# PSUM banks for the experts of a two-layer kernel: gates, ups, logits and transposes apart, projections in two banks, six row buffers, later output stores

## The chip, the cores and the metric

The kernel runs on one core of one Trainium2 chip, as one program that computes two layers. The metric is the device time of one execution in microseconds (us); the median of three runs is compared.

## The reference, cut to what matters

The program has many stages. The change touches the last one, which takes `x` of shape (8, 512, 256), runs a tanh recurrence over its 512 time steps, and feeds the states to a mixture of 16 experts, of which each token uses two:

```python
xW = jnp.einsum('ntd,dh->nth', x, Wx) + b
def step(h_prev, xw_t):
    h_next = jnp.tanh(xw_t + h_prev @ Wh)
    return (h_next, h_next)
_, hs = jax.lax.scan(step, h0, jnp.swapaxes(xW, 0, 1))
...
def _mlp(x, wg, wu, wd):
    return jnp.einsum('bsi,id->bsd', jax.nn.silu(x @ wg) * (x @ wu), wd)
router_logits = jax.nn.sigmoid(x @ gate_w + gate_b)
expert_values, expert_indices = jax.lax.top_k(router_logits, k=TOP_K)
expert_values = expert_values / jnp.sum(expert_values, axis=-1, keepdims=True)
...
return x + _mlp(x, shared_wg, shared_wu, shared_wd) + expert_weighted
```

The second `x` is the recurrence's output, and `expert_weighted` is the sum of the two chosen experts' `_mlp`, each times its value. The layer's input is added once more. All of it is in 32-bit floats.

## The kernel before, in words

The last stage is `rnn_moe` (L1565). Its loop over the 512 steps issues a step of the recurrence (`rnn_step`, L1262) and then at most one piece of other work on TensorE. In a step, TensorE (PE) multiplies the state with `wh` (L1273) into one of two small tiles `pg` and seeds the next step's tile with the projected input (L1257); ScalarE (ACT) takes the tanh (L1277); VectorE (DVE) transposes the result into `ring` (L1278), from which the next step's matmuls read. So a step is a loop PE, ACT, DVE, PE.

The order is written out by hand for PE, ACT and DVE (`manual_schedule`, L1664). Generators yield 1 when they have put a piece on PE and 0 when not. What a piece leaves for ACT and DVE goes into `later`, and `consume()` (L1630) issues it in the next step, behind that step's tanh and transpose. The kinds of pieces are:

- `rnn_project` (L1238): the input's projection for 16 time steps, 31 times, two pieces each. Both matmuls (L1247) accumulate into `px`; DVE adds the bias into `xw` (L1249).
- `chunk` (L1312): for 16 finished time steps (128 tokens), 32 times. The logits' matmul (L1327) and two transposes (L1337) write one tile `po`, the logits in columns 256 to 271, the transposes in columns 0 to 255; DVE and ACT turn the logits into `rl` (L1331, L1332), ACT copies the transposed rows to `hr` (L1342). Then come the shared expert's gate (L1348, L1350) and up (L1352), both into halves of one tile `pw`, ACT's sigmoid and DVE's two multiplies (L1356, L1357, L1361), and the down projection with the residual (L1365, L1369).
- `rank` (L1382): after a block of chunks (blocks of 6, 8, 11 and 7), DVE ranks the tokens by expert, and GpSimd (POOL) scatters the rows to a buffer `xs` in device memory, grouped by expert in tiles of 128 rows (L1455).
- `tiles` (L1467): 27, 31, 37 and 29 tiles for the four blocks, 124 in all, three pieces each: gate, up, down. `fetch` (L1473) loads a tile's expert weights `w` (384 KB) and rows `x` (128 KB) on SP's queue. `turn` (L1480) transposes half of the next tile's rows in the same piece as a gate or an up; `gate(m, 0)` and `gate(m, 1)` (L1490) write the gate and the up of tile m into the two halves of one tile `pg` of tag `gu` (L1493, L1496). ACT's sigmoid (L1501) and DVE's multiply (L1502) read the gate, DVE's second multiply reads the up (L1509). `down` (L1511) multiplies with the third weight; ACT copies the result to `y` (L1517), and SP stores it to `ys` (L1518).
- `collect` (L1541): POOL gathers each token's two rows from `ys` (L1550), DVE adds them to `acc` with their values (L1558), and SP stores `acc` to the output (L1562), 32 stores in all.

A chunk's piece goes first, otherwise a tile's (L1674). Gathers and scatters advance beside it. When the steps are over, the rest runs without them (L1678); this is called the tail here. Of the 124 tiles, 65 have had their store issued when the recurrence ends.

PSUM pools, each tile a whole bank: `psx` one (L1611), the recurrence two (L1612), `pxt` one for the row transposes (L1616), `pgu` two for gates and ups (L1617), `pd` two for `po`, `pd` and `py` (L1618). That is all eight. Dependencies are kept by bank: an instruction that writes a bank waits for all that read it before, whatever the columns.

SP and POOL are not in the hand-written order: a scheduler places their instructions by when buffers come free. Weights have seven buffers (`M.wp`, L1607), rows four (`M.sp`, L1606), the gathered rows six. Each DMA of SP's also waits for the eighth DMA before it.

Of the kernel before, what the change touches and what calls it, by code (L numbers as in the profile page):

```python
# [9 lines left out]
F32 = mybir.dt.float32  # L10
I32 = mybir.dt.int32
U32 = mybir.dt.uint32
AF = mybir.ActivationFunctionType
# [5 lines left out]
P = 128  # L19
B = 8  # L20
S = 512
D = 256
# [1215 lines left out]
def rnn_project(K, M):  # L1238

    ahead = chunk_x(K, M, 1, "xp")  # L1240
    for n in range(1, S // XB):
        xc = ahead
        if n + 1 < S // XB:
            ahead = chunk_x(K, M, n + 1, "xp")
        px = M.psx.tile([P, D], F32, name="px", tag="px")
        for k in range(2):
            K.nc.tensor.matmul(px, xc[:, k], M.wx[:, k, :], start=(k == 0), stop=(k == 1))  # L1247
            if k == 1:
                M.later(lambda n=n, px=px: K.nc.vector.tensor_tensor(M.xw[:, n, :], px, M.rbias, ALU.add))  # L1249
            yield 1  # L1250
# [30 lines left out]
class Experts:  # L1281
# [30 lines left out]
    def chunk(self, c, ring):  # L1312

        K, M, NE = self.K, self.M, self.NE
        nc, mm, later = K.nc, K.nc.tensor.matmul, M.later
        t0 = (self.first + c) * XB
        hT = M.hp.tile([P, 2, B, XB], F32, name="hT", tag="hT")
        for k in range(2):
            nc.gpsimd.tensor_copy(hT[:, k], ring[:, :, k, 0:B].rearrange("p t b -> p b t"))
        xc = chunk_x(K, M, t0 // XB, "xc")  # L1320
        hk = [hT[:, k].rearrange("p b t -> p (b t)") for k in range(2)]
        yield 0
        yield 0
        po = M.pd.tile([P, D + NE], F32, name="po", tag="pd")
        pr, pt = po[:, D:], po[:, 0:D].rearrange("p (k t) -> p k t", k=2)
        for k in range(2):
            mm(pr, hk[k], M.wr[:, k, :], start=(k == 0), stop=(k == 1))  # L1327
        rl = M.sp.tile([P, NE], F32, name="rl", tag="rl")

        def logits():  # L1330
            nc.vector.tensor_tensor(rl, pr, M.rb, ALU.add)  # L1331
            nc.scalar.activation(rl, rl, AF.Sigmoid)  # L1332

        later(logits)
        yield 1
        for k in range(2):
            nc.tensor.transpose(pt[:, k, :], hk[k], K.ident)  # L1337
        hr = M.ap.tile([P, D], F32, name="hr", tag="hr", bufs=16)
        self.hr.append(hr)

        def turned():
            nc.scalar.copy(hr, po[:, 0:D])  # L1342
            nc.vector.max(out=self.top[:, c, :], in_=rl)
            nc.vector.max_index(out=self.topi[:, c, :], in_max=self.top[:, c, :], in_values=rl)

        later(turned)
        pw = M.pgu.tile([P, 2, P], F32, name="pw", tag="gu")
        mm(pw[:, 0], M.wg[:, 0, :], hk[0], start=True, stop=False)  # L1348
        yield 1
        mm(pw[:, 0], M.wg[:, 1, :], hk[1], start=False, stop=True)  # L1350
        for k in range(2):
            mm(pw[:, 1], M.wu[:, k, :], hk[k], start=(k == 0), stop=(k == 1))  # L1352
        a = M.sp.tile([P, P], F32, name="a", tag="a")

        def act():
            nc.scalar.activation(a, pw[:, 0], AF.Sigmoid)  # L1356
            nc.vector.tensor_tensor(a, pw[:, 0], a, ALU.mult)  # L1357

        later(act)
        yield 1  # L1360
        later(lambda: nc.vector.tensor_tensor(a, pw[:, 1], a, ALU.mult))  # L1361
        yield 0
        yield 0
        pd = M.pd.tile([P, D], F32, name="pd", tag="pd")
        mm(pd, a, M.wd, start=True, stop=False)  # L1365
        yield 1
        pj = pd.rearrange("p (j k r) -> p k j r", j=4, k=2)
        for k in range(2):
            mm(pj[:, k], xc[:, k], K.ident, start=False, stop=(k == 1))  # L1369
        acc = M.ap.tile([P, D], F32, name="acc", tag="acc", bufs=27)  # L1370
        self.acc.append(acc)
        later(
            lambda: nc.vector.tensor_tensor(
                acc.rearrange("p (j k r) -> p j k r", j=4, k=2),
                pd.rearrange("p (j k r) -> p j k r", j=4, k=2),
                hr.rearrange("p (k j r) -> p j k r", j=4, k=2),
                ALU.add,
            )
        )
        yield 1  # L1380
# [86 lines left out]
    def tiles(self):  # L1467

        K, M, NT = self.K, self.M, self.NT
        nc, mm, later = K.nc, K.nc.tensor.matmul, M.later  # L1470
        W, X, G, A, T = {}, {}, {}, {}, {}

        def fetch(m):  # L1473
            W[m] = M.wp.tile([P, 768], F32, name="w", tag="w")
            row = nc.sync.value_load(self.wrow[0:1, m : m + 1], min_val=0, max_val=(self.NE - 1) * P)
            nc.sync.dma_start(out=W[m], in_=M.experts[bass.ds(row, P), :])
            X[m] = M.sp.tile([P, D], F32, name="x", tag="x")
            nc.sync.dma_start(out=X[m], in_=self.xs[m * P : (m + 1) * P, :])

        def turn(m, k):  # L1480
            if k == 0:
                T[m] = M.pxt.tile([P, 2, P], F32, name="pt", tag="xt"), M.sp.tile([P, 2, P], F32, name="xT", tag="xT")
            pt, xT = T[m]
            nc.tensor.transpose(pt[:, k, :], X[m][:, k * P : (k + 1) * P], K.ident)
            later(lambda: nc.scalar.copy(xT[:, k, :], pt[:, k, :]))
            if k == 1:
                T.pop(m)
                X[m] = xT

        def gate(m, g):  # L1490

            if g == 0:
                G[m] = M.pgu.tile([P, 2, P], F32, name="pg", tag="gu")  # L1493
            pg = G[m]
            for k in range(2):
                mm(pg[:, g], W[m][:, k * D + g * P : k * D + (g + 1) * P], X[m][:, k, :], start=(k == 0), stop=(k == 1))  # L1496
            if g == 0:
                a = A[m] = M.sp.tile([P, P], F32, name="ea", tag="ea")

                def silu():  # L1500
                    nc.scalar.activation(a, pg[:, 0], AF.Sigmoid)  # L1501
                    nc.vector.tensor_tensor(a, pg[:, 0], a, ALU.mult)  # L1502

                later(silu)
            else:
                X.pop(m)
                G.pop(m)
                a = A[m]
                later(lambda: nc.vector.tensor_tensor(a, pg[:, 1], a, ALU.mult))  # L1509

        def down(m):  # L1511
            py = M.pd.tile([P, D], F32, name="py", tag="pd")
            M.last = mm(py, A.pop(m), W.pop(m)[:, 2 * D : 3 * D], start=True, stop=True)

            def keep():
                y = M.sp.tile([P, D], F32, name="y", tag="y")
                nc.scalar.copy(y, py)  # L1517
                nc.sync.dma_start(out=self.ys[m * P : (m + 1) * P, :], in_=y)  # L1518

            later(keep)  # L1520

        for m in range(3):
            fetch(m)
        for k in range(2):
            turn(0, k)
        yield 1
        for m in range(NT + 1):
            for n in range(3):
                if n < 2 and m < NT:
                    gate(m, n)  # L1530
                    if m + 1 < NT:
                        turn(m + 1, n)
                    yield 1
                if n == 2:
                    if m:
                        down(m - 1)
                    if m + 3 < NT:
                        fetch(m + 3)
                    yield 1

    def collect(self):  # L1541

        K, M, nc = self.K, self.M, self.K.nc
        C, Y = self.C, {}
        for c in range(C + 2):
            for i in range(2):
                if c < C:
                    y = Y[c, i] = M.sp.tile([P, D], F32, name="yg", tag="yg", bufs=6)
                    self.paced(
                        nc.gpsimd.indirect_dma_start(  # L1550
                            out=y, out_offset=None, in_=self.ys[:, :], in_offset=bass.IndirectOffsetOnAxis(ap=self.row[:, c, i : i + 1], axis=0)
                        )
                    )
                    for _ in range(2 if M.left else 0):
                        yield 0
                if c > 1:
                    acc = self.acc[c - 2]
                    nc.vector.scalar_tensor_tensor(acc, Y.pop((c - 2, i)), self.tw[:, c - 2, i : i + 1], acc, ALU.mult, ALU.add)  # L1558
                yield 0
            if c > 1:  # L1560
                t0 = (self.first + c - 2) * XB
                nc.sync.dma_start(out=M.out[:, t0 : t0 + XB, :], in_=acc)  # L1562
# [293 lines left out]
```

## Time and profile before

| | us |
|---|---|
| median of 3 runs | 4574.04 (4570.07 to 4579.55) |
| the profiled execution | 4707.05 |
| its span, first to last instruction | 4705.1 |
| recurrence in it, first to last tanh | 3774.3 to 4515.8 |
| tail in it | 4516 to 4705 |
| busy in the span: PE | 3502.3 (74%) |
| busy in the span: DVE | 2148.3 (46%) |
| busy in the span: ACT | 1313.6 (28%) |
| busy in the span: POOL | 897.2 (19%) |

The profile is of one execution, longer than the timed ones, and covers all stages. For this change its totals say little; the stage has to be cut out by windows. A group is named by its line in the kernel, its engine, and output and inputs by tile. "PEld" is the weight load that precedes a matmul. A wait is written as the instruction that waited and the one that released it. A 32-bit matmul stands as two records, so "x4" is two matmuls.

### The profile page before, as it was taken

To read this page: it belongs to the slowest core of one execution; us is meant where nothing else is said; L and a number is where in the kernel's file an instruction comes from. 1 tells how busy PE (TensorE), PEld (TensorE's weight loads), DVE (VectorE), ACT (ScalarE), POOL (GpSimd) and SP (SyncE) were. 2 spreads that over 40 slices of the span, in tenths; PEclk is the share of its full clock that TensorE was granted. 3 is DMA by queue.
4 is the path that set the end of the run, shared out by engine and by line. 5 is a ranking of instruction groups with operands and counts; after the bars stand their busy time and mean duration, and the time that the engine had idled before them with its cause. 6 is when DMAs were issued, how large, how long until landed. Compare 5 with 4: busy or idle time off the path is not lost.

```text
span 4705.1 us, 122302 instructions
## 1 busy us (share of the span) xinstructions
PE 3502.3 (74%) x51550; PEld 2195.2 (47%) x51550; DVE 2148.3 (46%) x7641; ACT 1313.6 (28%) x4703; POOL 897.2 (19%) x1534
## 2 busy tenths in 40 slices
PE   8700067777766767578889999999999977888685
PEld 5500044444444444345545555555555545656464
DVE  3300045555554444434547666667666622332332
ACT  2100012222222222133434334433433311323132
POOL 0077500000000000042102222222222211020312
PEclk9855589999999999989999999999999987989698
DMA  2100000000000000100000000000000021333267
GB/s 77 37 1 1 0 16 17 17 17 12 12 3 3 3 3 3 54 26 19 9 2 1 1 1 1 1 1 1 1 1 1 7 88 45 115 113 107 88 202 216
DMA packets 103895, 155.55 MB, mean 33 GB/s; under 512 B 21264, under 2 KB 73776, under 8 KB 102960
## 3 DMA queue, kind: packets, MB, share of 16 engines
q1 hardware_dynamic: 72064, 108.46, 7.6%
q0 software_dynamic: 18432, 23.28, 1.7%
q10 hardware_dynamic: 12848, 15.99, 1.0%
q8 instruction: 404, 6.62, 0.6%
q14 instruction: 147, 1.20, 0.1%
HBM read 107.82 MB, written 41.02 MB: 32 GB/s over the span
## 4 chain that ended last, share of the span: by engine, by line
PE 53%; DVE 21%; ACT 9%; another core or an unknown queue 7%; issue 7%; DMA 1%; ACTq 1%; POOL 0%; SPq 0%; DVEq 0%; POOLq 0%
PE pga L629 9%; PE pg L1273 5%; DVE G L635 4%; PE pe L1107 4%; PE po L1161 3%; PE pg L1496 3%; PE pt L1146 3%; PE pp L1074 3%; ACT X L636 3%; PE pv L1092 3%; ACT th L645 2%; PE px L1177 2%; DVE pr L641 2%; DVE ring L646 2%
## 5 line engine op out<-in xcount | busy, mean ns | idle before, releaser
L629 PE MATMUL pga<-wh,ring 128*8 128x192 f32 x8176 | 427.8, 327 | 382.7 <-DVE ring L646 367.6
L629 PEld LDWEIGHTS pga<-wh,ring 128*8 128x8 f32 x8176 | 172.0, 88 | 633.1 <-DVE ring L646 579.1
L1278 DVE STREAM_TRANSPOSE ring<-h 128x64 f32<-128x64 f32 x512 | 125.6, 245 | 524.3 <-ACT h L1277 509.6
L635 DVE STREAM_TRANSPOSE G<-pga 128x192 f32<-128x192 f32 x512 | 196.5, 384 | 364.6 <-PE pga L629 364.6
L1127 ACT ACTIVATE sm<-sm,nm 128x388 f32<-128x388 f32 (+3 forms) x512 | 283.6, 555 | 252.4 <-DVE nm L1123 250.9
L636 ACT ACTIVATE X<-G 128x48 f32<-128x48 f32 x512 | 124.1, 242 | 813.5 <-DVE G L635 806.2
L441 PE MATMUL pA<-ohl,ohh 128*32 128x16 f32 x512 | 29.9, 215 | 369.6 <-DVE ohl L438 198.2
L1074 PE MATMUL pp<-hn,wqkv 128*128 128x512 f32 x512 | 280.9, 689 | 11.0 <-DVE hn L1060 11.0
L1273 PE MATMUL pg<-wh,ring 128*8 128x64 f32 x8176 | 231.5, 238 | 71.5 <-DVE ring L1278 63.1
L1277 ACT ACTIVATE h<-pg 128x64 f32<-128x64 f32 x512 | 114.2, 223 | 575.6 <-PE pg L1273 526.6
L420 POOL DMA_INDIRECT gath<-sdr,idx x256 | 253.1, 989 | 99.4 <-issue 77.7
L606 PE MATMUL pga<-xw,ident 128*8 128x192 f32 x4096 | 261.6, 326 | 0.5 <-DVE xw L600 0.5
L1107 PE MATMUL pe<-kt,qt 32*128 32x132 f32 (+3 forms) x2048 | 257.9, 470 | 0.1
L1136 POOL COPY pme<-sm 128x4 f32<-128x4 f32 x512 | 126.5, 247 | 651.6 <-DVE sm L1132 647.2
L1146 PE MATMUL pt<-ident,sm 128*128 128x128 f32 x1280 | 210.6, 286 | 45.7 <-DVE eT L1148 45.5
L1146 PEld LDWEIGHTS pt<-ident,sm 128*128 128x128 f32 x1280 | 150.6, 145 | 165.0 <-DVE eT L1148 77.2
L1496 PE MATMUL pg<-xT,w 128*128 128x128 f32 x992 | 176.7, 302 | 67.1 <-DVE ea L1502 59.1
L1161 PE MATMUL po<-eT,v 128*64 128x128 f32 x2560 | 205.5, 281 | 17.2 <-DVE rr L1078 15.3
L1273 PEld LDWEIGHTS pg<-wh,ring 128*8 128x8 f32 x8176 | 128.2, 94 | 191.7 <-DVE ring L1278 137.0
L629 PE MATMUL pgo<-wh,ring 128*8 128x64 f32 x8176 | 207.7, 219 | 0.0
L1132 DVE TENSOR_SCALAR sm<-sm,rc 128x388 f32<-128x388 f32 (+3 forms) x512 | 199.9, 433 | 5.2
L441 PEld LDWEIGHTS pA<-ohl,ohh 128*32 128x32 f32 x512 | 28.4, 156 | 371.8 <-DVE ohl L438 199.4
(490 smaller groups left out, 7018.2 us busy)
## 6 DMA issues: line engine op xcount, KB each, us to landing
w<-in_experts_dram SPq DMA_DIRECT2D x124, 384.0 KB
x<-xs SPq DMA_DIRECT2D x124, 128.0 KB
ys<-y SPq DMA_DIRECT2D x124, 128.0 KB
xs<-zero ACTq DMA_DIRECT2D x2, 4736.0 KB
w<-in_ada_w_dram SPq DMA_DIRECT2D x16, 512.0 KB
gath<-sdr,idx POOLq DMA_INDIRECT x256
out_dram<-acc SPq DMA_DIRECT2D x32, 128.0 KB
wqkv<-in_w_qkvT_dram SPq DMA_DIRECT2D x1, 3072.0 KB
```

Of the source, the lines that this page charges most:

```text
L420: nc.gpsimd.indirect_dma_start(out=gath[:, c : c + 1], out_offset=None, in_=sdr[:, :], in_offset=bass.IndirectOffsetOnAxis(ap=idx[:, c : c ...
L606: mm(pga[t % 2][32 * j : 32 * j + B], pick[:, tt, :], xw[:, j * 256 : j * 256 + 192], start=True, stop=False)
L629: mm(dst[32 * j : 32 * j + B], hp, wh[:, k, j * 256 + lo : j * 256 + hi], start=False, stop=(k == 1))
L635: nc.vector.transpose(G[:, 0:3].rearrange("p g k b -> p (g k b)"), a.rearrange("p g n -> p (g n)"))
L636: nc.scalar.activation(X[:, 0:3], G[:, 0:3, :, 0:B], AF.Tanh)
L1074: mm(pp, T.wqkv[:, k, 0 : 2048].rearrange("p (i g h n) -> p i g h n", i=2, g=4, h=2)[:, i, g, h], self.hn[b][:, k, :], start=(k == 0), sto ...
L1107: mm(pe[a][:, 0 : w - lo], q[r, h, at], k[r, h, lo:w], start=(h == 0), stop=(h == 1))
L1127: nc.scalar.activation(sm[a][:, 0:w], sm[a][:, 0:w], AF.Exp, bias=nm[:, a : a + 1], scale=-1.0, accum_out=su[:, a : a + 1])
L1146: nc.tensor.transpose(pt[:, j, :], sm[a][:, 4 + j * P : 4 + (j + 1) * P], K.ident)
L1161: mm(po[64 * f : 64 * f + 64, pr, :], v[:, j, 64 * a : 64 * a + 64], eT[a][:, j, :], start=(j == 0), stop=(j == c))
L1273: mm(pg[32 * j : 32 * j + B], hp, M.wh[:, k, 64 * j : 64 * j + 64], start=False, stop=(k == 1))
L1496: mm(pg[:, g], W[m][:, k * D + g * P : k * D + (g + 1) * P], X[m][:, k, :], start=(k == 0), stop=(k == 1))
```

## The change

There are five edits, all in the last stage. The gate and the up of an expert tile, and those of a chunk's shared expert, get a tile of tag `gu` each in place of the halves of one; the pool still has two banks. A chunk's logits and transposes get a tile of tag `pd` each in place of parts of `po`; the chunk's second multiply moves into the same `later` as the first. The projections take the bank of `psx` and that of `pxt` in turn; the row transposes that use `pxt` come only after the projections. The rows `x` get six buffers in place of four. `collect` yields once more before each output store.

```diff
-        px = M.psx.tile([P, D], F32, name="px", tag="px")
+        px = (M.psx, M.pxt)[n % 2].tile([P, D], F32, name="px", tag=("px", "xt")[n % 2])
...
-        po = M.pd.tile([P, D + NE], F32, name="po", tag="pd")
-        pr, pt = po[:, D:], po[:, 0:D].rearrange("p (k t) -> p k t", k=2)
+        pr = M.pd.tile([P, NE], F32, name="pr", tag="pd")
...
+        pt = M.pd.tile([P, 2, P], F32, name="pt", tag="pd")
...
-            nc.scalar.copy(hr, po[:, 0:D])
+            nc.scalar.copy(hr, pt.rearrange("p k t -> p (k t)"))
...
-        pw = M.pgu.tile([P, 2, P], F32, name="pw", tag="gu")
-        mm(pw[:, 0], M.wg[:, 0, :], hk[0], start=True, stop=False)
+        pw = [M.pgu.tile([P, P], F32, name="pw", tag="gu")]
+        mm(pw[0], M.wg[:, 0, :], hk[0], start=True, stop=False)
         yield 1
-        mm(pw[:, 0], M.wg[:, 1, :], hk[1], start=False, stop=True)
+        mm(pw[0], M.wg[:, 1, :], hk[1], start=False, stop=True)
+        pw.append(M.pgu.tile([P, P], F32, name="pw", tag="gu"))
         for k in range(2):
-            mm(pw[:, 1], M.wu[:, k, :], hk[k], start=(k == 0), stop=(k == 1))
+            mm(pw[1], M.wu[:, k, :], hk[k], start=(k == 0), stop=(k == 1))
...
-            nc.scalar.activation(a, pw[:, 0], AF.Sigmoid)
-            nc.vector.tensor_tensor(a, pw[:, 0], a, ALU.mult)
+            nc.scalar.activation(a, pw[0], AF.Sigmoid)
+            nc.vector.tensor_tensor(a, pw[0], a, ALU.mult)
+            nc.vector.tensor_tensor(a, pw[1], a, ALU.mult)
 
         later(act)
         yield 1
-        later(lambda: nc.vector.tensor_tensor(a, pw[:, 1], a, ALU.mult))
...
-            X[m] = M.sp.tile([P, D], F32, name="x", tag="x")
+            X[m] = M.sp.tile([P, D], F32, name="x", tag="x", bufs=6)
...
         def gate(m, g):
 
+            pg = M.pgu.tile([P, P], F32, name="pg", tag="gu")
+            for k in range(2):
+                mm(pg, W[m][:, k * D + g * P : k * D + (g + 1) * P], X[m][:, k, :], start=(k == 0), stop=(k == 1))
             if g == 0:
-                G[m] = M.pgu.tile([P, 2, P], F32, name="pg", tag="gu")
-            pg = G[m]
-            for k in range(2):
-                mm(pg[:, g], W[m][:, k * D + g * P : k * D + (g + 1) * P], X[m][:, k, :], start=(k == 0), stop=(k == 1))
...
+            def part():
+                if g == 0:
+                    nc.scalar.activation(a, pg, AF.Sigmoid)
+                nc.vector.tensor_tensor(a, pg, a, ALU.mult)
+
+            later(part)
...
                 yield 0
+            yield 0
             if c > 1:
                 t0 = (self.first + c - 2) * XB
                 nc.sync.dma_start(out=M.out[:, t0 : t0 + XB, :], in_=acc)
```

## The prediction

> **What bounds the kernel now.** I read the page first: it says that PE holds over half of the chain that ended last, but gives averages over many stages, and the diff touches only the last one. So I cut that stage out with the busy time of windows. Its columns are the window, its length, the busy time of PE, PEld, DVE, ACT and POOL with counts, TensorE's granted clock, DMA share and GB/s.
>
> ```profile
> 3774.00:4516.00 742.00, 591.43 (x13823) 413.57 (x13824) 223.40 (x1016) 185.57 (x875) 130.25 (x258) 0.87 0.29 90
> 4516.00:4600.00 84.00, 62.99 (x409) 52.47 (x408) 26.03 (x102) 34.79 (x130) 18.02 (x20) 0.98 0.86 258
> 4600.00:4680.00 80.00, 54.53 (x304) 43.61 (x302) 23.60 (x73) 29.55 (x101) 17.01 (x18) 0.91 0.80 244
> ```
>
> The first row is the recurrence: 512 steps, 742 us, DMA mostly idle, no engine full. The others are the tail, where expert tiles run without a recurrence and DMA is nearly full. What holds the recurrence is its own loop, PE to ACT to DVE to PE, plus whatever a slice of other work (a "piece") puts between. The waits of window 3774 to 4516 (who waited for whom: us, times, longest) name the pieces that stall it:
>
> ```profile
> PEld pg L1496 <- DVE ea L1502: 50.8, 53, 1.9
> ...
> PEld po L1337 <- DVE rl L1331: 24.9, 31, 1.5
> PE px L1247 <- DVE xw L1249: 22.1, 24, 1.1
> ```
>
> Up waits for the gate's multiply, the chunk's transposes for its logits, a projection for the evacuation of the one before. The timeline (start, length, instruction, idle before it) shows what one costs: PE works in order, so the next step's recurrence, ready when `ring` is written, stands behind the waiting piece.
>
> ```profile
> 4000.78 0.22 ACT L1277 ACTIVATE h<-pg 128x64 f32<-128x64 f32 x1 [0.98 <-PE pg L1273]
> 4001.20 0.29 DVE L1502 TENSOR_TENSOR ea<-pg,ea 128x128 f32<-128x128 f32 x1
> 4001.55 0.71 PE L1496 MATMUL pg<-xT,w 128*128 128x128 f32 x4 [0.73 <-DVE ea L1502]
> 4002.78 0.22 ACT L1277 ACTIVATE h<-pg 128x64 f32<-128x64 f32 x1 [1.45 <-PE pg L1273]
> 4003.86 0.22 ACT L1277 ACTIVATE h<-pg 128x64 f32<-128x64 f32 x1 [0.70 <-PE pg L1273]
> 4005.06 0.22 ACT L1277 ACTIVATE h<-pg 128x64 f32<-128x64 f32 x1 [0.72 <-PE pg L1273]
> ```
>
> From tanh to tanh: 2.00 us with an up piece, 1.08 with a down, 1.20 with a gate, which issues exactly an up's matmuls. In the tail, the waits of 4516 to 4705 give the same stall 31 times, and the chain of waits shows late row loads:
>
> ```profile
> PEld pg L1496 <- DVE ea L1502: 25.2, 31, 1.7
> ```
> ```profile
> 4564.39 0.71 PE pg L1496 x4
> ...
> 4566.78 0.71 PE pg L1496 x4
> ...
> 4637.83 5.56 DMA x<-xs
> ...
> 4665.22 3.59 DMA x<-xs
> ```
>
> Before about 4600 a tile takes 2.39 us (4564.39 to 4566.78); later loads of x, 3.6 to 5.6 us from issue to landing, set the pace.
>
> **The Trainium skill.** "PSUM — Partial Sum Buffer", section "PSUM bank collisions raise a hardware error", says to guard PSUM by bank and quadrant, not by address: another address in the same bank and quadrant still collides. The trace agrees that this is done: up writes columns 128 to 255 of the bank whose columns 0 to 127 DVE reads, and waits (53 times). "TensorE: Matmul & The Clock Gate", "The HAM clock gate", says that the clock halves when PE is little used. The 20 us windows from 4390 to 4430, with recurrence and gathers but no tiles, show 0.50, those with tiles 1.00; so less stalling can't lower the clock. "Perfetto Trace Analysis", "What "DMA-bound" means", names the issuing sequencer as a bound apart from the transfer engines; SP's timeline from 4628 to 4640 agrees: issues almost back to back, 2.14 us from one weight load to the next (4628.13 to 4630.27).
>
> **The change, part by part.**
>
> *Gate and up in banks of their own.* Removed: 53 waits in the recurrence. An up step becomes like a gate step, 2.00 to 1.20: 53 x 0.80 = 42.4 us. Each `gu` bank is written again only a tile later, so I cost the new waits for its earlier reader at nothing; their cover is three steps (1.20 + 1.20 + 1.08 = 3.5 us), against 1.2 from the gate's end (4000.26) to that of DVE's multiply (4001.49).
>
> *Logits and transposes apart.* 31 waits. Around 4011 the step takes 1.74 us (tanh 4010.40 to 4012.14); its 0.6 us of PE work without the wait fits a 1.05 to 1.20 step. I take 0.65 each: 20.2 us. `pd` now gives three tiles a chunk; by turns the readers are done a step before.
>
> *Projections in two banks.* 24 waits; pairs of steps of 2.03 and 1.08 become two of 1.08 (tanh at 3794.62, 3796.65, 3797.73): 24 x 0.95 = 22.8 us. Cover: POOL's copies of `xp`, 0.53 us a pair, with a 2.16 us pair left.
>
> *Chunk's shared gate and up.* They take both `gu` banks, where one stood free before. In the built order of PE, 11 of the 32 chunks are followed one step later by an expert gate or up whose bank the chunk's multiply still holds. That is a stalled up step again: 11 x 0.80 = 8.8 us added. Bounds: 0, if ACT is early, and 1.9 us each, the longest wait above; queued behind it is the recurrence. DVE's second multiply comes a step earlier, 0.29 us behind the first, and ends before the next `h`.
>
> Recurrence: 42.4 + 20.2 + 22.8 - 8.8 = **76.6 us saved**. Bounds: 55, if half-clock stretches return little, to 94 (the weight-load waits above are 50.8 + 24.9, with 27.0 for px, less 8.8).
>
> *The tail.* The waits' 0.82 us leave a tile's PE work at 2.39 - 0.82 = 1.57 us. What is late next is the feed. A tile moves 384 + 128 + 128 KB, 655,000 bytes; window 4550 to 4570 moved 303 GB/s at a DMA share of 0.97. At some 300 GB/s a tile needs 2.18 us. Then SP's order: with six row buffers the built order puts SP's row loads only four tiles ahead of the y store from store 79 on; before, six ahead until 90 and four from about 100. With four ahead, three tiles pass in 0.9 (store to load issue) + L + 1.9 (transpose to store, 2.71 at 4563.53 to 4566.24, less 0.82). L of 3.6, 4.3 and 5.6 gives 2.13, 2.37 and 2.80 us a tile. So: about 10 tiles at 2.18 for 2.5, -3; 19 tiles at 2.37 for 2.39, 0 (-5 to +8); the block's boundary, where x of tile 97 now goes out behind store 95, +4; the last 25 tiles, where SP is back to back but the loop is 0.27 shorter, -4; output stores behind their DVE add, -2 (SP waited 1.9 us for DVE there). Sum **-5**, bounds -25 (all 31 waits returned) and +16.
>
> *Stores a piece later* also stretches `collect` from six steps a chunk to seven; POOL has that slack in the recurrence, and the 25 us after the last tile keep their 14 gathers. Nothing.
>
> The profiled execution took 4707.05 us, its span 4705.1; minus 82 it would be 4623. The median is 133 us lower than the profiled time, and I cannot place that. I take the same microseconds off the median, since steps are chains of latencies (in proportion it would be 80): 4574.0 - 76.6 - 5 = **4492**.
>
> **Rivals.**
> *Tail pays too.* For it: the 31 stalls. Against: DMA share 0.86. 4574.0 - 76.6 - 25 = 4472.
> *Tail loses.* The shallower order of loads costs: four-ahead at L = 5.6 and the boundary, +16: 4513. For it: the built order; against: x lands in 3.6 when DMA is calmer.
> *The up wait only moves.* If each gate came to wait for the same bank's earlier reader, the 42.4 would stay: 4534. The three-piece distance speaks against it.
> *Slower.* SP's in-order queue starves the tail: place, the last 59 tiles, 2.76 us each now (163 us); it decides once a tile takes over 2.76 + 76.6/59 = 4.06 us. By the loop L must pass 3 x 4.06 - 2.8 = 9.4 us. At 4.5 us a tile: 4574 - 76.6 + 103 = 4600. Loads of 5.6 us at most speak against it.
>
> **How the numbers follow.** Forecast 4492: 0.52. Tail pays 0.17, tail loses 0.17, wait moves 0.06, slower 0.05; 0.03 for losses that just cancel the gain. About 0.2% (9 us) is what a measurement can tell from no change. Faster 0.52 + 0.17 + 0.17 + 0.06 = 0.92, same 0.03, slower 0.05. The first three hold 0.86; with recurrence bounds, 4460 to 4522 should hold 8 in 10.
>
> **What would show it.** Right: waits of PE for `ea` near 11 in the recurrence, none for `rl` and `xw`; up steps of 1.20; a recurrence near 665 us instead of 742; a tail near 184 instead of 189, row loads on its chain from block 2's tiles on. Wrong: up steps still at 2.00 (wait moved), or tiles over 2.8 us before the output stores begin.

## The result, and the profile after

The median fell from 4574.7 to 4499.9 us (four runs each), a ratio of 0.984 with a 95% interval of 0.982 to 0.986. That is 74.8 us less. The forecast was 4492, 82 less.

The two profiled executions on record can't be set against each other. Their spans differ by 202 us (4705.1 and 4502.7), and 86 of these lie ahead of the recurrence, where the kernels are the same: it begins at 3774.3 in one and at 3688.3 in the other. Both kernels were therefore run once more on one chip. There before took 4713.1 us and after 4636.6, ratio 0.985 (0.983 to 0.987): 76.5 us less, nearly the same gain at a time 137 us longer. So the time went with the chip, or with the hour at which it was used, and the gain hardly did. The record names no chip for the first two traces; by its span, that of before belongs with the longer ones. All traces called "second" below are from the one chip on which both kernels were run again. The busy time of windows of the second trace of after, with columns as in the prediction; the first row is its recurrence, the others are its tail:

```profile
3779.00:4444.00 665.00, 577.87 (x13823) 407.84 (x13824) 226.93 (x1016) 185.58 (x875) 130.93 (x258) 0.90 0.33 100
4444.00:4527.00 83.00, 66.82 (x402) 56.60 (x400) 25.36 (x101) 35.74 (x129) 17.35 (x20) 0.92 0.82 250
4527.00:4608.00 81.00, 56.38 (x308) 47.33 (x308) 23.79 (x74) 30.02 (x103) 17.71 (x19) 0.87 0.82 249
4608.00:4633.00 25.00, 0.00 (x0) 0.00 (x0) 6.78 (x14) 0.00 (x0) 13.23 (x14) 0.56 0.40 115
```

The recurrence of the second trace of before is its first row:

```profile
3779.00:4517.00 738.00, 586.16 (x13823) 410.58 (x13824) 223.39 (x1017) 185.94 (x875) 130.78 (x258) 0.88 0.30 90
```

So 738 us became 665 with ACT and POOL as busy as before, DVE 4 us more and PE 8 us less: nearly all that went is waiting. The tail was 189.7 us (4516.7 to 4706.4) and still is (4443.8 to 4633.5). On this chip all of the gain lies in the recurrence, and the 5 us forecast for the tail didn't come. Whom PE waits for there, in the second trace of after (us, times, longest):

```profile
PEld pg L1273 <- DVE ring L1278: 152.5, 306, 8.5
...
PEld pg L1495 <- DVE a L1358: 10.6, 11, 1.0
...
PEld pt L1485 <- ACT xT L1486: 2.9, 4, 1.0
```

The waits for `ea`, `rl` and `xw`, which stood at 50.8, 24.9 and 22.1 us (50.1, 24.4 and 22.1 in the second trace of before), are gone from the list. In their place is the predicted wait for the chunk's multiply, 11 times, and what PE waits for most is the recurrence's own `ring`. The timeline of a gate step and the up step after it, in the same trace:

```profile
4008.02 0.22 ACT L1277 ACTIVATE h<-pg 128x64 f32<-128x64 f32 x1 [0.86 <-PE pg L1273]
...
4009.20 0.71 PE L1495 MATMUL pg<-xT,w 128*128 128x128 f32 x4
4009.22 0.23 ACT L1277 ACTIVATE h<-pg 128x64 f32<-128x64 f32 x1 [0.71 <-PE pg L1273]
4009.34 0.27 ACT L1504 ACTIVATE ea<-pg 128x128 f32<-128x128 f32 x1
...
4009.50 0.27 ACT L1486 COPY xT<-pt 128x128 f32<-128x128 f32 x1
...
4009.82 0.14 PEld L1485 LDWEIGHTS pt<-ident,x 128*128 128x128 f32 x1
...
4010.56 0.22 ACT L1277 ACTIVATE h<-pg 128x64 f32<-128x64 f32 x1 [0.79 <-PE pg L1273]
```

The up's matmul now starts at 4009.20, ahead of the sigmoid (4009.34) that it used to wait behind. But the step takes 1.34 us (4009.22 to 4010.56), not the gate's 1.20 (4008.02 to 4009.22). The row transpose in the same piece is loaded at 4009.82, right after ACT's copy of the other half of `pt` ends (4009.50 + 0.27): the two halves share the bank of `pxt`, and ACT makes the sigmoid first.

In the tail the wait for `ea` is gone too, and rows stand in its place. The waits of 4444 to 4633 in the second trace of after, and of 4517 to 4706 in that of before:

```profile
PEld pt L1485 <- DMA x<-xs: 39.3, 26, 3.0
```
```profile
PEld pg L1496 <- DVE ea L1502: 23.8, 29, 1.0
PEld pt L1484 <- DMA x<-xs: 23.2, 16, 2.6
```

24 us of waits for `ea` went and 16 us more for rows came: one wait took the place of another. The chain of waits of the tail (start, length, what) has row loads from tile 84 on, which is in block 2; before, it had them only from 4602, in block 3:

```profile
4478.12 5.74 DMA x<-xs
...
4491.97 4.08 DMA x<-xs
...
4499.02 4.24 DMA x<-xs
...
4506.23 5.30 DMA x<-xs
```

### The profile page after: what moved, and what is told of

The parts are those of the page before. It is cut to its first block, busy times and chain, and to the rows that moved or that the text cites. A ratio compares the mean times of both kernels' runs of the same rounds, so it can differ in the third digit from the quotient of the medians.

```text
span 4502.7 us, 122270 instructions
## 1 busy us (share of the span) xinstructions
PE 3477.5 (77%) x51550; PEld 2186.1 (49%) x51550; DVE 2156.9 (48%) x7641; ACT 1315.9 (29%) x4703; POOL 889.8 (20%) x1534
## 4 chain that ended last, share of the span: by engine, by line
PE 53%; DVE 21%; ACT 8%; issue 8%; POOL 6%; DMA 2%; ACTq 1%; SPq 0%; DVEq 0%; POOLq 0%
PE pga L629 10%; POOL gath L420 5%; PE pe L1107 4%; DVE G L635 4%; PE pg L1273 4%; PE po L1161 3%; PE pt L1146 3%; PE pp L1074 3%; ACT X L636 3%; PE pv L1092 3%; PE pg L1495 3%; ACT th L645 3%; PE px L1177 2%; DVE pr L641 2%; DVE ring L646 2%
## 5 line engine op out<-in xcount | busy, mean ns | idle before, releaser
L1273 PE MATMUL pg<-wh,ring 128*8 128x64 f32 x8176 | 221.7, 229 | 56.0 <-DVE ring L1278 52.1
L420 POOL DMA_INDIRECT gath<-sdr,idx x256 | 243.0, 949 | 99.5 <-issue 77.7
L629 PEld LDWEIGHTS pgo<-wh,ring 128*8 128x8 f32 x8176 | 169.6, 90 | 53.6
L1148 DVE COPY eT<-pt 128x128 f32<-128x128 f32 (+3 forms) x384 | 176.0, 484 | 37.0 <-PE pt L1146 36.4
```

Source lines behind the costliest of these rows:

```text
L420: nc.gpsimd.indirect_dma_start(out=gath[:, c : c + 1], out_offset=None, in_=sdr[:, :], in_offset=bass.IndirectOffsetOnAxis(ap=idx[:, c : c ...
L629: mm(dst[32 * j : 32 * j + B], hp, wh[:, k, j * 256 + lo : j * 256 + hi], start=False, stop=(k == 1))
L1273: mm(pg[32 * j : 32 * j + B], hp, M.wh[:, k, 64 * j : 64 * j + 64], start=False, stop=(k == 1))
```

## The experiments

The runs are from four chips. Two gave the kernel before at 4713 to 4714 us; two others, used for the last runs made (output stores where they were, loads seven tiles ahead, the matmul of no use, and all that helped), at 4577. Each ratio is to before on its own chip; its interval is about ±0.002, 9 us. After itself was not timed on every chip: "on after" compares with 4636.6 or 4499.9, whichever was measured where before took about as long. Terms of the recurrence are therefore read from the traces, as lengths from first to last tanh. Such a length comes again within about 4 us: 737.6 and 741.4 in the two traces of before, and 665.0 in the second of after against 665.8 and 668.1 in two kernels below that change only output stores or row buffers. What is smaller than that is read step by step.

**Both kernels again, without an edit.**

> The kernel before once more, for a second trace of it. The first trace's span was 4705.1 us against a median of 4574. Place theory: 86 of these 131 us lie ahead of the recurrence, the other 45 in the recurrence, whose stretches without tiles ran at a granted clock of 0.50: the new trace has a span near 4573, a recurrence near 697 instead of 742, and no 0.50 stretches. Rival: the recurrence takes 742 again with its 0.50 stretches, and the whole excess lies ahead of it; then the change saves 115 us in the recurrence and loses 40 elsewhere. Time against itself: ratio 1.000.

Measured: 4714.9 us, ratio 1.000 (0.999 to 1.001), span 4706.4, recurrence 737.6. The recurrence came out about as the rival had it, but neither expectation held, since 4715 and not 4574 is the usual time there. The first trace was no outlier: this is what before takes on such a chip, its lean stretches (steps of the recurrence without expert tiles, at a low granted clock) included.

> The changed kernel once more, for a second trace. Recurrence 627 us within 5, tail 187 within 5, if the first trace was a usual one; median 4500. If the granted clock in stretches without tiles (0.75 in the first trace) is a matter of chance, it will be another value here and the recurrence differs by more than 5.

Measured: 4636.6 us; recurrence 665.0, tail 189.7. The recurrence is 38 us longer than in the first trace, so that one can't be compared with before's. What differs between such pairs is in the last section.

**Gates and ups back into one bank, the chunk's too.** The chunk's second multiply comes one step later again, as in before.

```diff
-            pg = M.pgu.tile([P, P], F32, name="pg", tag="gu")
+            if g == 0:
+                G[m] = M.pgu.tile([P, 2, P], F32, name="pg", tag="gu")
+            pg = G[m][:, g]
...
-        pw = [M.pgu.tile([P, P], F32, name="pw", tag="gu")]
+        pq = M.pgu.tile([P, 2, P], F32, name="pw", tag="gu")
+        pw = [pq[:, 0], pq[:, 1]]
```

> The changed kernel with gate and up of an expert tile, and those of the chunk, in halves of one bank again. Sum of waits: +42.4 for the up steps (2.00 instead of 1.20, about 53 times), -8.8 for the chunk's 11 waits, tail unchanged because the feed sets it: 4500 + 34 = 4534. Rival (clock): stalled steps also bring back a lower granted clock in the recurrence, 4550 or more. Rival (tail pays): the 0.82 us a tile return in the tail too, 59 tiles at up to 0.4 each, 4555.

Measured: 4666.8 us, 0.989, +30 on after; recurrence 698.2 (+33.2, by the sum +33.6), tail 186.9. The wait is back as it was:

```profile
PEld pg L1497 <- DVE ea L1508: 52.5, 53, 1.9
```

The tail doesn't lose by it (186.9 us against 189.7), so neither rival's sum came. But the stalls are not hidden: there are 35 of them in the tail, and where they stand they set the pace. The chain of waits there has no row load from 4510 to 4555; it goes round the gate's sigmoid, its multiply and the up, one tile in 2.39 us (4524.51 to 4526.90):

```profile
4524.51 0.29 ACT ea L1507
...
4524.82 0.30 DVE ea L1508
...
4525.17 0.71 PE pg L1497 x4
...
4525.99 0.43 PE py L1514 x2
4526.42 0.46 PE pg L1497 x4
4526.90 0.29 ACT ea L1507
```

With the stalls, SP's order asks for rows eight tiles ahead of the store until store 87; without them, in after, only four ahead from store 77 on. So this undo changes two things in the tail at once, stalls against late rows, and together they are no loss: tiles 77 to 95 take 44.1 us here and 48.1 in after.

**Only the chunk's back into one bank** (the last three lines of that diff, and the second multiply where it was before).

> The changed kernel with the chunk's shared gate and up in halves of one bank again, the experts' in two. Sum of waits: the 11 waits of PE behind DVE's second multiply go, 8.8 us less: 4491. Rival: they are 10.6 us in all by the list of waits but 1.0 at most each and partly hidden beside the step: 4500, no change. Rival: the chunk's up waits for its own gate's multiply, as before, in the step of its 2 + 4 records: slower by up to 32 x 0.3 = 10, 4510.

Measured: 4633.3 us, 0.984, -3 on after, within the interval; recurrence 660.9, 4.1 less, which alone is no more than two traces differ by. Step by step it is plain. The 11 steps that wait in after for the chunk's first multiply take 22.2 us there, 12.8 in the second trace of before, and 13.6 here: the waits cost 9.4, about the 8.8 of the prediction, and 8.6 of that come back. But the waits of this recurrence have a new line:

```profile
PEld pg L1495 <- DVE a L1362: 4.3, 5, 0.9
```

Five other up steps now wait for the chunk's second multiply, which comes a step later again; four of them become 1.96 us instead of 1.34. From here to the run above, the experts' gates and ups alone make 698.2 - 660.9 = 37.3 us.

**Projections back into one bank.**

```diff
-        px = (M.psx, M.pxt)[n % 2].tile([P, D], F32, name="px", tag=("px", "xt")[n % 2])
+        px = M.psx.tile([P, D], F32, name="px", tag="px")
```

> The changed kernel with all projections in the one bank of psx again. Sum of waits: +22.8 us against the changed kernel (24 waits of 0.95), all of it in the first 130 steps of the recurrence. By the step lengths of the two traces (projection steps 100.9 against 74.7 us in all) it should be 26. Rival: the second bank only brings the wait for POOL's copies into view (27.0 us of PE weight loads waited for xp before), so undoing it costs under 10.

Measured: 4666.2 us, 0.990, +30 on after; recurrence 689.0 (+24.0), all of it in the first 85 steps (97.8 to 122.2 us), where some 27 steps are longer by 0.95 in the median. Its waits:

```profile
PEld px L1247 <- POOL xp L1234: 26.6, 25, 1.1
PE px L1247 <- DVE xw L1249: 21.7, 24, 1.0
```

The two lines are one stall: PE reaches the projection late, loads late, and the load is put down to `xp`. With the second bank both went together, so the rival, which took the 27 us for a wait of their own, falls.

**Logits and transposes back into one bank.**

```diff
-        pr = M.pd.tile([P, NE], F32, name="pr", tag="pd")
+        po = M.pd.tile([P, D + NE], F32, name="po", tag="pd")
+        pr, pt = po[:, D:], po[:, 0:D].rearrange("p (k t) -> p k t", k=2)
```

> The changed kernel with a chunk's logits and transposes in one bank again. Sum of waits: +20.2 us (31 waits of 0.65), transposing steps of 1.74 in place of 1.10. Rival: apart, the third tile per chunk makes a piece wait for the bank of pd somewhere else, so that the undo costs less than half of it, under 10.

Measured: 4662.7 us, 0.989; recurrence 680.1, +15.1. (Its profiled execution was among its shorter ones, and the median is 26 above after's, so the trace is the smaller of two readings.) The wait is back 31 times:

```profile
PEld po L1337 <- DVE rl L1331: 24.3, 31, 1.6
```

In stretches with tiles a transposing step becomes 1.74 us in place of 1.10, 0.64 each, as estimated. In the lean stretches, where the granted clock is 0.50 and a chunk's two transposes take 0.69 us instead of 0.44, it is mostly 0.2 to 0.5.

**Four row buffers.**

```diff
-            X[m] = M.sp.tile([P, D], F32, name="x", tag="x", bufs=6)
+            X[m] = M.sp.tile([P, D], F32, name="x", tag="x")
```

> The changed kernel with four row buffers in place of six. As predicted, the six buffers are what makes the built order of SP shallow in the tail, so four would give the loads back and the tail up to 5 us. Rival: the built order is as shallow with four buffers, because it follows from gates and ups having banks of their own (it is as deep as before only where these share a bank), so the time is the same within 3 us.

Measured: 4640.4 us, 0.984, no change. The built order of SP, that is the order of its DMAs in the finished program, explains it: with four buffers the row loads stand four tiles ahead of the y store from store 75 on, with six from 77; with gates and ups in one bank (and six buffers) they stand eight ahead until 87. So the shallow order comes from the gate and up banks, to which the scheduler adapts SP, and not from the row buffers.

**Output stores where they were.**

```diff
                 yield 0
-            yield 0
             if c > 1:
```

> The changed kernel without the further yield of collect ahead of an output store. As predicted the edit does nothing: the same within 3 us, and the stretch from the last tile's store to the end stays 26 us. Rival: without it SP waits for DVE's add again at each output store in the tail (1.9 us was seen once), so that the last 24 tiles take up to 2 more each time, 10 to 20 us slower.

Measured: 4501.6 us, 0.984; recurrence 627.0 (626.9 in the first trace of after), and 25.7 us from the last tile's store to the end (after 25.7). Its tail is 182.6 us against 187.5 in the first trace of after, all of it in tiles 97 to 124 (82.9 and 88.1); but the second trace of after has 82.9 there too, so this is how much one trace differs from another. No effect of the edit shows.

**Output stores issued by ACT.**

```diff
-                nc.sync.dma_start(out=M.out[:, t0 : t0 + XB, :], in_=acc)
+                nc.scalar.dma_start(out=M.out[:, t0 : t0 + XB, :], in_=acc)
```

> The changed kernel with the output stores issued by ACT in place of SP. If SP's queue sets the last 24 tiles (3.4 us a tile with an output store nearly every other tile, against 2.5 for the tiles before, which have none), they take about 2.5 to 2.7 each: 18 to 22 us less. Rival: bytes and the latency of row loads set them, and the gathers that come at the same time: no change within 5. Rival: ACT, held up by DVE's add ahead of each store, delays the sigmoids and row copies: slower by up to 10.

Measured: 4632.6 us, 0.983 (0.981 to 0.985), not told from after's by time. In the trace the tiles 101 to 124 take 64.6 us in place of 72.6 (70.9 to 72.7 in the other changed kernels on these two chips). So SP's issues are 6 to 8 of the 18 to 22 us expected of them; with them gone a tile still takes 2.7 us, its rows landing 4 to 5 us after issue.

**Loads seven tiles ahead.**

```diff
-        with K.tc.manual_schedule(engines={E.PE, E.Activation, E.DVE}):
+        with K.tc.manual_schedule(engines={E.PE, E.Activation, E.DVE, E.SP}):
...
-        for m in range(3):
+        for m in range(6):
             fetch(m)
...
-                    if m + 3 < NT:
-                        fetch(m + 3)
+                    if m + 6 < NT:
+                        fetch(m + 6)
```

> The changed kernel with SP's instructions in the hand-written order too, and each tile's loads asked for six tiles ahead: seven tiles of loads stand ahead of each y store instead of four. If the four-tile order is what costs time in the tail (row loads landing 4 us after issue, tiles 77 to 95 at 2.5 us), these come down to the 2.2 that 655,000 bytes at 300 GB/s need, 6 us less, and the last 24 tiles also gain up to 8; against that the first loads of the last block are issued only behind store 95, +6. Sum -8. Rival: the transfers' bytes set the tail already, then it's 0 to +6.

Measured: 4487.3 us, 0.981 (0.979 to 0.983); its interval meets after's, but the trace is plain: the tail is 171.0 us, in place of 187.5 in the first trace of after and 182.6 in the kernel with output stores where they were, which ran on the same chip. The windows of the last block's tiles, first this kernel, then that one:

```profile
4377.00:4459.00 82.00, 59.28 (x348) 48.84 (x348) 25.15 (x80) 29.68 (x116) 20.84 (x22) 0.92 0.90 287
```
```profile
4381.00:4472.00 91.00, 62.78 (x348) 51.65 (x347) 25.62 (x80) 33.63 (x117) 20.76 (x22) 0.89 0.83 252
```

The same records in 82 us and in 91 (96 in the first trace of after, at 238 GB/s); DMA share and rate rose from 0.83 and 252 to 0.90 and 287. So after's tail had room: its loads were asked for too late. Tiles 77 to 95 fall from 43.0 us to 37.2, the 6 us expected, and the boundary costs what was expected too (store 95 to 96: 14.0 against 8.1). The surprise is the last block, where stores 97 to 124 take 67.4 us in place of 82.9. The run also takes SP out of the scheduler's hands, and that alone was not tried.

**A matmul of no use in steps without a piece.** It is extra work; the outputs don't depend on it.

```diff
-                advance(chunks) or advance(big)
+                if not (advance(chunks) or advance(big)):
+                    idle = M.pd.tile([P, D], F32, name="idle", tag="pd")
+                    K.nc.tensor.matmul(idle, K.ident, M.wd, start=True, stop=True)
```

> The changed kernel with one matmul of no use (128x128 by 128x256, its result read by nobody) in each of the about 79 steps of the recurrence that have no piece. If the stretches without tiles run at a granted clock of 0.50 because PE has little to do there, the clock stays at 1.00: steps of 1.24 become 1.08 (a step with a down piece), about 13 us less, and other pieces in those stretches gain too, up to 38 in all (the first trace of the changed kernel, at 0.75 there, had a recurrence shorter by that). Rival: the clock doesn't follow the work, or the matmuls themselves stand ahead of the recurrence: 0 or up to 5 us slower.

Measured: 4476.2 us, 0.978 (0.976 to 0.980), clear of after's 0.982 to 0.986. The windows of two lean stretches, first of this kernel, then the same steps in the first trace of after:

```profile
3784.00:3856.00 72.00, 71.54 (x1736) 46.28 (x1735) 26.27 (x126) 17.10 (x78) 16.73 (x28) 1.00 0.22 75
4184.00:4246.00 62.00, 61.70 (x1497) 40.00 (x1497) 25.31 (x106) 15.52 (x70) 40.95 (x51) 1.00 0.46 150
```
```profile
3786.00:3870.00 84.00, 62.46 (x1672) 45.32 (x1660) 26.32 (x126) 17.27 (x78) 16.70 (x28) 0.74 0.19 64
4199.00:4269.00 70.00, 52.02 (x1411) 37.76 (x1415) 25.37 (x107) 15.55 (x70) 40.34 (x49) 0.78 0.42 134
```

The clock went from 0.74 and 0.78 to 1.00, and the stretches lost 12 and 8 us though PE does more. In the Trainium skill, "TensorE: Matmul & The Clock Gate", section "The HAM clock gate", says that the idle state is the throttled one and that activity releases it. The trace agrees, and shows that activity without a use will do: 88 such matmuls here. Nor does it take a long idle gap to lose the clock. In the first of these stretches of after, PE is never idle for more than 0.7 us, and the clock alternates between 1.00 and 0.50, mostly for 10 us each:

```profile
3827.80:3838.00 10.20, 6.34 (x247) 4.24 (x246) 3.58 (x17) 2.28 (x11) 3.85 (x6) 1.00 0.53 170
3838.00:3848.30 10.30, 8.55 (x170) 6.60 (x174) 2.08 (x11) 1.94 (x9) 4.24 (x6) 0.50 0.53 194
```

Of the 20 us by which the recurrence is shorter, 19 are in steps with a chunk's pieces; the filled steps themselves gain about 2.

**All that helped, together**: the chunk in one bank, loads seven ahead, output stores on ACT, the matmul of no use, and the gate's `later` behind the transpose's:

```diff
-                    gate(m, n)
+                    part = gate(m, n)
                     if m + 1 < NT:
                         turn(m + 1, n)
+                    later(part)
```

> A kernel meant to beat both, of five edits on the changed one: the chunk's shared gate and up in one bank again (measured alone: about 4 us less in the recurrence), the gate's sigmoid issued behind ACT's copy of the transposed rows (an up step of 1.34 becomes 1.20 because the second transpose no longer waits for that copy: about 49 x 0.14 = 7 less), loads seven tiles ahead of the stores with SP in the hand-written order (11 less alone), output stores on ACT (5 less alone), and the matmul of no use in steps without a piece (24 less alone). Sum -51, ratio to before about 0.972. Rival: the last two edits of the tail share their gain (the bytes are the bound for both), and ACT's queue holds up its copies: only -40, 0.975.

Measured: 4451.4 us (4450.6 to 4456.9), before 4576.7, ratio 0.973 (0.971 to 0.974). It beats both kernels, after's 4499.9 by 48 us of the 51 expected. Its recurrence is 589.4 us, from 3689.9 to 4279.4. The windows of the recurrence and of the tail's tiles (columns as before), then the timeline of an up step:

```profile
3690.00:4279.00 589.00, 578.10 (x13988) 400.93 (x13992) 228.35 (x1016) 186.18 (x873) 131.49 (x258) 0.99 0.36 112
4279.00:4345.00 66.00, 54.62 (x378) 44.03 (x371) 23.75 (x95) 30.58 (x116) 14.59 (x17) 1.00 0.86 273
4345.00:4425.00 80.00, 61.51 (x348) 49.16 (x348) 25.18 (x80) 30.29 (x116) 21.42 (x22) 0.87 0.89 288
```
```profile
3882.96 0.22 ACT L1277 ACTIVATE h<-pg 128x64 f32<-128x64 f32 x1 [0.98 <-PE pg L1273]
3883.08 0.26 ACT L1486 COPY xT<-pt 128x128 f32<-128x128 f32 x1
3883.22 0.29 ACT L1504 ACTIVATE ea<-pg 128x128 f32<-128x128 f32 x1
...
3883.39 0.14 PEld L1485 LDWEIGHTS pt<-ident,x 128*128 128x128 f32 x1
...
3884.16 0.22 ACT L1277 ACTIVATE h<-pg 128x64 f32<-128x64 f32 x1 [0.64 <-PE pg L1273]
```

PE is busy for 578 of 589 us in the recurrence, in part with work of no use. The copy now stands ahead of the sigmoid, the transpose starts 0.46 us after the up's matmul (3882.93) in place of 0.62, and the step is 1.20, as 52 of this kernel's 66 such steps are; the swap was not tried alone. The tail is 171.3, as with deep loads alone: the stores on ACT add nothing to them.

## Why the prediction was right

The terms in us, the recurrence by undoing each part (traces from the two longer chips), the tail by the issue times of the y stores in the two second traces. Each is the difference of two traces, good to about 4 us:

| step | predicted | measured |
|---|---|---|
| experts' gates and ups | -42.4 | -37.3 |
| chunk's shared gate and up | +8.8 | +4.1 (the 11 steps alone: +9.4) |
| logits and transposes | -20.2 | -15.1 |
| projections | -22.8 | -24.0 |
| recurrence, sum | -76.6 | -72.3; direct 737.6 - 665.0 = -72.6 |
| tail: to store 76 | -3 | 30.1 to 25.0, -5.1 |
| tail: stores 77 to 95 | 0 | 43.6 to 48.1, +4.5 |
| tail: boundary, store 96 | +4 | 6.4 to 7.8, +1.4 |
| tail: 97 to 124, output stores | -6 | 83.8 to 82.9, -0.9 |
| tail: after that | 0 | 25.8 to 25.9, +0.1 |
| sum | -82 | -72.6; by the medians -74.8 and -76.5 |

- **Luck in the sum.** The recurrence was forecast at 665 us and measured at 665.0. That close a hit is chance: the start was 737.6 and not 742, the saving 72.6 and not 76.6, and within the saving two terms that were 5 too large stand against one that came out 5 smaller by its undo. That the undone parts add up to within 0.3 of the direct difference is closer than traces repeat, too.
- **Gates and ups.** The mechanism held: 53 waits gone, none moved to the gate, and they return when it is undone. The size was off because an up step became 1.34 us, not 1.20: 0.66 each by the steps that changed. "An up step becomes like a gate step" missed that its transpose writes a bank which ACT still reads. That wait had stood behind the 0.8 us one, and came next once that was gone.
- **Chunk's gate and up.** 11 waits, as read from the built order, and the price was right: 9.4 us more in those steps than before. The 4.1 of the table is a net figure, since undoing the edit brings five waits for the second multiply.
- **Logits and transposes.** 0.64 us each where tiles run, as costed, but not in the lean stretches; the bound of 55 had named this, the value taken had not.
- **Projections.** Right in count, price and cover.
- **Clock.** It didn't fall. On one chip it rose only from 0.88 to 0.90 over the recurrence.
- **Tail.** Right that the feed takes over, and that row loads come onto the chain from block 2 on; the 5 us of gain didn't come (189.7 before and after). The loop formula with the landing times seen (about 4.2 us) gives 7.0 us for three tiles, and tiles 85 to 87 took 7.1 (stores at 4490.97 and 4498.07); over 77 to 95 the mean was 2.53 and not 2.37, because some rows landed only after 5.3 to 5.8. "With six row buffers the built order puts SP's row loads only four tiles ahead" was wrong in its cause: the gate and up banks do it. It cost the forecast nothing, since the order itself was read from the changed kernel.
- **The 133 us** that the prediction could not place go with the chip or the hour of the run. The gain was 76.5 us where before takes 4713 and 74.8 where it takes 4575; whether it goes with the chip's time can't be told, since that would make 2 us.
- **Rivals.** "Tail pays too" falls with 189.7 us before and after, and so does "tail loses" by 16. The tail's stalls did cost time, though: without them, and with loads asked for seven ahead, tiles 77 to 95 took 37.2 us, on a chip of the shorter kind where after takes 42.9. "The up wait only moves" falls with up steps of 1.34. The slower one needed tiles above 4.06 us; they took 2.8 on average (163.8 us for 59).

## What to carry to other kernels

In a build that keeps dependencies by bank, as this one does, two results that share a PSUM bank are one resource: a reader of one half makes PE wait with the other, and in a loop of latencies such a wait came to 0.64 to 0.95 us a step here, though no engine was full. When a wait goes, look in the same piece for the next reader of a bank, in the order in which its engine reaches it; swapping two ACT instructions made good what a bank had left. When compute gets shorter and the time stays, look at how early the loads are asked for: here the edit to the compute had itself changed the scheduler's order of loads, from six tiles ahead to four, and the tail gained nothing until they were asked for seven ahead.

## What the runs showed of the hardware beyond what was expected

- **Two kinds of chip, or of hour.** Before takes 4713 and 4714 us on two chips and 4577 on two others. Each chip was used in one batch of runs, so the chip and the hour can't be told apart. The stage with 256 gathers by POOL (L420), ahead of the recurrence, takes 371 us in the second trace of after and 303 in the first. In the recurrence, take the steps with little on PE (no piece, or a chunk's down or an expert's down). Those in which a gather or scatter of POOL's starts take 1.68 us on average in the second trace (48 steps) and 1.11 in the first (51); those in which none starts take 1.12 and 1.10. The clock is not the reason: among steps at a granted clock of 1.00, those with one take 1.56 and 1.07. So in the longer runs an indirect DMA goes with almost 0.6 us more in its step, 48 x 0.57 = 27 of the 38 us between those recurrences. Why was not tried.
- **A clock that can be kept.** One 128x128 by 128x256 matmul in each of 88 otherwise empty steps held the granted clock at 1.00 where it had been 0.74 to 0.78, and paid 24 us by the medians (4500 to 4476). Without it the clock fell to 0.50 again and again in a stretch where PE had no idle gap over 0.7 us.
- **The same bytes, sooner asked.** DMA moved 287 GB/s with loads seven tiles ahead and 238 to 252 with four, in the same work.
